# Two-stream cross-attention: the second-to-last batch's prompt values weighted on GpSimd and VectorE within the last batch, its projection placed earlier, and the last output stored in halves

## The chip, the cores and the metric

The kernel runs on one core of one Trainium2 chip. A core has TensorE (matrix products, results in the accumulation memory PSUM), VectorE, ScalarE and GpSimd (elementwise work in the on-chip memory SBUF; in this kernel VectorE and ScalarE read PSUM, GpSimd does not), and SyncE, which issues most transfers (DMA). Each engine works through its own queue in order, and waits on semaphores for the others. The metric is the time of one execution in device microseconds; the profile gives the time line of one profiled execution. In the profile's rows PE is TensorE, PEld its weight loads, DVE VectorE, ACT ScalarE, POOL GpSimd, SP SyncE; a q behind an engine's name is its sequencer, which issues and waits.

## The reference

There are 8 batches of 112 query rows with 320 channels (20 heads of 16), and for each batch 371 text tokens and 4 prompt tokens of 512 channels. For every head:

```
q = x @ W_q;  k, v = text @ W_k, text @ W_v;  k_ip, v_ip = prompts @ W_k_ip, prompts @ W_v_ip
probs_t  = softmax(q k^T / 4)                        # 112 x 371
text_out = probs_t @ v
qsem     = normalised(probs_t @ text)                # 512 channels
sem      = qsem @ normalised(prompts)^T              # 112 x 4
probs_ip = softmax(q k_ip^T / 4 + 0.5 * sem) * spatial_mask
out      = (text_out + probs_ip @ v_ip) @ W_out + b_out + x
```

All in float32. The norm of probs_t @ text is taken through the Gram matrix of the text tokens, so that the 512 channels are never formed for each query.

## The kernel before

**Tiling.** A batch's 20 heads are worked in five groups of four (`groups`, g = 0 to 4). For each group, `scores` makes the four score matrices, `probabilities` takes the maximum (VectorE, L678), the exponential (ScalarE, L682) and sends the probabilities through a DMA into the ring `xg` (L689); `transposed` turns them on VectorE (L701); `multiplied` takes the products with Gram matrix, prompt logits, a column of ones and values (`product`, L713) in 12 blocks; `reduced` (VectorE, L766) and `value_sums` (ScalarE, L740) take the results out of PSUM. In the last batch a part of the reductions goes through `shared`: copies on ScalarE (L750, L751), products on GpSimd (L755), sums on ScalarE (L759). `placed` (GpSimd, L632) puts a group's values beside the Gram matrix into the tile `u`; it must wait until TensorE is done with what stood there.

**Ends of batches.** What remains of a batch after its five groups is in `finish`, a generator that is advanced in pieces, each at a place written out by hand, between the products of the following batch. It divides the text part by the sums (`divided`, L812, GpSimd), makes the prompt weights w (L828 to L846), adds the weighted prompt values to the text part, turns the result (`ps_a`, copied to `aT`), projects it with W_out (`ps_o`, L896), adds input and bias (L902, VectorE) and stores it (L905).

For batches 0 to 5 the weighted prompt values are made on GpSimd: the batch's four prompt values are loaded to all 112 partitions (`prompt_values`, L591, 560 KB), multiplied by w (L874, 1280 elements a partition), and added up (L880 to L882). For batch 6 (`bd` given) it is done on TensorE: w is turned (L851), copied (L853), and multiplied with a table `bd` of 80 rows, one for each head and prompt, that holds the prompt's values in the head's own channels and zero elsewhere (L858, L865). `prompt_values_by_head` and `load_prompt_values_by_head` bring two such tables, for batches 6 and 7, through DRAM, and `own_channels` (L615, L618) clears what isn't a head's own.

**The last batch.** Batch 7 has no batch behind it, and its end is `ending`: the first 16 heads are divided and turned early; `bd` for batch 7 is turned (`ps_bT`, L963) and multiplied with W_out (`ps_bw`, L974), so that w, once turned (L1012), is multiplied with the projected table (L1015) into the same PSUM tile in which the text part's projection (L990) stands. One sum (L1019) and one store (L1020) follow.

**Order.** All five engines' queues are in the order of the program text. The order around the change is in `behind` (for batch 6's last group, where `finish(6)` is begun), in the loop over g of the last batch, and in the lines after it, which advance `ending(7)` (called `last`) and `finish(6)` (called `before`) in turns: of `finish(6)`, the turning of w comes after the first piece of `ending`, the two products into `ps_a` after the third, the projection L896 after the sixth, the sum L902 after the seventh, the store L905 after everything. GpSimd adds batch 7's input and bias (`with_bias`, L780) behind the cut of the tables in g = 1. PSUM tiles come from the pools mm, sc and qd; `bank(..., spare=True)` takes sc.

Of the kernel before, what the change touches and what calls it, by code (L numbers as in the profile page):

```python
# [20 lines left out]
def kernel(  # L21
# [209 lines left out]

    vipx = dram.tile([2, H, NIP, C], F32, tag="vipx", name="vipx", bufs=1)

# [362 lines left out]
    def prompt_values_by_head():  # L596

        nc.sync.dma_start(
            vipx,
            vipd[N - 2 * NIP :, :]  # L600
            .rearrange("(b n) c -> b n c", n=NIP)
            .unsqueeze(1)
            .to_broadcast([2, H, NIP, C]),
        )

    def load_prompt_values_by_head():
        t = io.tile([P, NT, E], F32, tag="ct", name="bd")
        st[B - 1]["xb"] = t[:S, 2, :C]
        bd = t[:HN, :2, :CP]
        nc.sync.dma_start(bd[:, :, :C], vipx.rearrange("b h n c -> (h n) b c"))  # L610
        return bd

    def own_channels(bd):

        nc.gpsimd.memset(bd[:, :, C:], 0.0)  # L615
        v = bd[:, :, :C].rearrange("p b (h d) -> p b h d", d=D)
        for sign, base in ((1, 0), (-1, NIP - 1)):
            nc.gpsimd.affine_select(  # L618
                out=v,
                in_=v,  # L620
                compare_op=ALU.is_ge,
                fill=0.0,
                base=base,
                pattern=[[0, 2], [-sign * NIP, H], [0, D]],
                channel_multiplier=sign,
            )
# [152 lines left out]
    def with_bias(b):  # L779
        nc.gpsimd.tensor_tensor(st[b]["xb"], x_sb[:, b, :], bias_sb, ALU.add)  # L780


    def finish(b, bd=None):

# [31 lines left out]
        if bd is not None:  # L816
            nc.vector.reciprocal(zr, z)
            divided()
        yield

        nc.scalar.activation(rn, rn, AF.Sqrt)
        nc.scalar.preload_act_table(AF.Exp)
        if bd is None:
            nc.vector.reciprocal(zr, z)
            divided()
        yield
# [21 lines left out]

        if bd is not None:
            ps = bank(f"ps_wT_{b}")  # L850
            nc.tensor.transpose(ps[:HN, :S], w.rearrange("s h n -> s (h n)"), ident[:S, :S])  # L851
            wT = work.tile([P, NE, TP], F32, tag="ctxT", name=f"wT_{b}")[:, 0, :S]
            nc.scalar.copy(wT[:HN], ps[:HN, :S])  # L853
            yield

            ps = bank(f"ps_a_{b}", spare=True)
            for i in range(NC):
                nc.tensor.matmul(  # L858
                    ps[:, i * S : (i + 1) * S],
                    attn[:, i * P : (i + 1) * P],  # L860
                    ident[:S, :S],
                    start=True,
                    stop=False,
                )
                nc.tensor.matmul(  # L865
                    ps[:, i * S : (i + 1) * S],
                    bd[:HN, i * P : (i + 1) * P],
                    wT[:HN],
                    start=False,
                    stop=True,  # L870
                )
        else:
            wv = work.tile([S, NIP, H, D], F32, tag="wv", name=f"wv_{b}", bufs=1)
            eng.tensor_tensor(  # L874
                wv,
                s["vip"],
                w.rearrange("p h n -> p n h").unsqueeze(3).to_broadcast([S, NIP, H, D]),
                ALU.mult,
            )
            eng.tensor_tensor(wv[:, :2], wv[:, :2], wv[:, 2:], ALU.add)  # L880
            eng.tensor_tensor(ah, ah, wv[:, 0], ALU.add)
            eng.tensor_tensor(ah, ah, wv[:, 1], ALU.add)  # L882
            yield

            ps = bank(f"ps_a_{b}", spare=True)
            for i in range(NC):
                nc.tensor.transpose(
                    ps[:, i * S : (i + 1) * S], attn[:, i * P : (i + 1) * P], ident[:S, :S]
                )
        aT = work.tile([P, NC, S], F32, tag="aT", name=f"aT_{b}")  # L890
        nc.scalar.copy(aT, ps[:, : NC * S].rearrange("p (i s) -> p i s", s=S))
        yield

        ps = bank(f"ps_o_{b}", spare=bd is not None)
        for i in range(NC):
# [13 lines left out]
    def ending(b, bd):  # L909
# [59 lines left out]

        ps_bw = bank("ps_bw")  # L970
        for i in range(NC):

            own = slice(i * RG, min((i + 1) * RG, HN))
            nc.tensor.matmul(  # L974
                ps_bw[own, :C], bT[:, i, own], wo_sb[:, i, :], start=True, stop=True
            )
        yield

        z2, rn = sm("z2"), sm("rn")
# [6 lines left out]

        turned_attention(range(FULL, NC))
        ps_o = bank(f"ps_o_{b}", spare=True)
        for i in range(NC):
            nc.tensor.matmul(  # L990
                ps_o[:S, :C], aT[:, i, :], wo_sb[:, i, :], start=(i == 0), stop=False
            )
        nc.vector.reciprocal(rn, rn)
# [20 lines left out]
        nc.scalar.copy(wT[:HN], ps[:HN, :S])  # L1014
        nc.tensor.matmul(ps_o[:S, :C], wT[:HN], bw, start=False, stop=True)  # L1015
        yield

        ob = work.tile([S, C], F32, tag="xb", name=f"ob_{b}", bufs=1)
        nc.vector.tensor_tensor(ob, ps_o[:S, :C], s["xb"], ALU.add)  # L1019
        nc.sync.dma_start(out[b], ob)  # L1020
        del st[b]
# [181 lines left out]
    def behind(n):  # L1203
# [73 lines left out]
        elif b % 2 == 0:  # L1277
# [6 lines left out]
            f(b - 1, 2)  # L1284
            run(("f", b), lambda: finish(b, bd=bd[:, 0]), 2)
        elif g == 1:
# [100 lines left out]
    drain(sums)  # L1387
    last = ending(b, bd[:, 1])
    next(last)
    run(before, None)  # L1390
    reduced(b, g, 0, 1)
    value_sums(b, g, 1)
    next(last)
    value_sums(b, g, 0, 1)
    reduced(b, g, 1)
    next(last)
    run(before, None)
    for _ in range(3):
        next(last)
    run(before, None)  # L1400
    next(last)
    run(before, None)
    drain(last)
# [44 lines left out]
```

## Time and profile before

| | |
|---|---|
| median of 3 runs | 428.86 us (424.92 to 431.55) |
| the profiled execution's own time | 426.6 us |
| its span, first to last instruction | 424.9 us |
| TensorE busy | 416.1 us, 98% |
| VectorE busy | 329.0 us, 77% |
| ScalarE busy | 185.9 us, 44% |
| GpSimd busy | 110.6 us, 26% |
| mean granted clock of TensorE | 0.997 |
| DMA | 64.27 MB, mean 151 GB/s |

All times in rows are from the span's start; the span leaves 1.7 us of the execution's own time outside. A row of the timeline reads: start, length, engine, line, operation, what it writes and reads, shape, count, and in brackets the idle time of the engine before it with what ended it. A row of the chain reads: start, length, what. A row of the stages reads: stretch, length, busy time of each engine with the count of instructions, granted clock, the DMA engines' share and rate.

### The profile page before, as it was taken

Reading aid. Unit: us, or ns where it says so; the run is one execution under the profiler, and the core shown is the slowest. Engines: PE = TensorE matmul, PEld = TensorE weight load, DVE = VectorE, ACT = ScalarE, POOL = GpSimd, SP = SyncE. Lnnn points to the kernel's source line nnn. Section 1 sums busy time; section 2 is a strip of 40 time slices with the busy share of each in tenths; the row PEclk is TensorE's granted clock in tenths of the full one; section 3 lists DMA queues with packets and bytes.
Section 4 is the critical chain, followed back from the end, with each engine's and each line's share of the span. In section 5 each row is a group of like instructions: output and inputs, shape, how many; then the busy total and the mean of one; then the engine's idle time right before and its main releaser. Section 6 shows DMA issues by size and latency. Waiting matters only on the chain.

```text
span 424.9 us, 14020 instructions
## 1 busy us (share of the span) xinstructions
PE 416.1 (98%) x5513; PEld 324.7 (76%) x5513; DVE 329.0 (77%) x681; ACT 185.9 (44%) x635; POOL 110.6 (26%) x271
## 2 busy tenths in 40 slices
PE   8999999999999999999999999999999999999995
PEld 8866586888677796879686887779776888777992
DVE  4055777877998887887889897797888897788963
ACT  3263243324633643424553454333633563356672
POOL 4303110031161342022061234003133226006440
PEclk9999999999999999999999999999999999999998
DMA  8677956778555656477645566586755435663400
GB/s 246 168 193 229 183 152 168 166 181 194 143 151 142 165 137 168 131 169 176 165 115 138 156 158 162 140 189 142 182 139 139 117 107 149 155 175 107 112 18 27
DMA packets 58254, 64.27 MB, mean 151 GB/s; under 512 B 19072, under 2 KB 52216, under 8 KB 58190
## 3 DMA queue, kind: packets, MB, share of 16 engines
q1 hardware_dynamic: 57498, 62.50, 58.8%
q8 instruction: 43, 0.70, 0.8%
q10 hardware_dynamic: 692, 0.89, 0.7%
q14 instruction: 21, 0.17, 0.1%
HBM read 18.67 MB, written 5.32 MB: 56 GB/s over the span
## 4 chain that ended last, share of the span: by engine, by line
PE 95%; DMA 1%; DVE 1%; ACT 1%; issue 0%; ACTq 0%; POOL 0%; SPq 0%; DVEq 0%; POOLq 0%
PE ps_qd L713 43%; PE ps_v L543 15%; PE ps_k L512 10%; PE ps_g L474 8%; PE ps_s L665 6%; PE ps_q L344 4%; PE ps_o L896 2%; PE ps_g L444 1%; DMA xg<-p 1%; PE ps_c L414 1%; PE ps_w L431 1%; PE ps_kv L280 1%; PE ps_k L526 1%; PE ps_k L503 1%; PE ps_x L336 0%
## 5 line engine op out<-in xcount | busy, mean ns | idle before, releaser
L713 PE MATMUL ps_qd<-u,xgT 32*112 32x232 f32 (+11 forms) x3840 | 218.1, 352 | 1.8 <-POOL u L632 1.3
L713 PEld LDWEIGHTS ps_qd<-u,xgT 32*112 32x112 f32 x3840 | 186.3, 172 | 33.1 <-issue 7.5
L701 DVE STREAM_TRANSPOSE xgT<-xg 128x768 f32<-128x768 f32 (+1 forms) x63 | 122.7, 1974 | 9.6 <-DMA xg<-p 9.1
L682 ACT ACTIVATE p<-ps_s,nmx 112x371 f32<-112x371 f32 x160 | 85.8, 585 | 50.1 <-DVE nmx L678 45.2
L766 DVE CUSTOM_DVE_ANT_0 junk<-ps_qd,p 112x371 f32<-112x371 f32 x150 | 81.2, 542 | 31.8 <-ACT pvs L740 10.9
L678 DVE TENSOR_REDUCE nmx<-ps_s 112x1 f32<-112x371 f32 x160 | 77.3, 536 | 22.3 <-PE ps_s L665 20.5
L632 POOL COPY u<-vr 128x64 f32<-128x64 f32 x120 | 26.9, 237 | 196.6 <-PE ps_qd L713 112.2
L543 PE MATMUL ps_v<-wv_sb,ctxT 128*128 128x384 f32 (+1 forms) x192 | 63.8, 479 | 0.3 <-ACT kT L519 0.3
L665 PE MATMUL ps_s<-kT,qm 32*112 32x375 f32 (+1 forms) x320 | 61.0, 486 | 0.0
L543 PEld LDWEIGHTS ps_v<-wv_sb,ctxT 128*128 128x128 f32 x192 | 35.3, 190 | 21.2 <-ACT kT L519 1.2
L740 ACT COPY pvs<-ps_qd 112x21 f32<-112x21 f32 x150 | 21.9, 199 | 62.1 <-DVE ss L766 60.9
L512 PE MATMUL ps_k<-ctxT,wk_sb 128*128 128x371 f32 x136 | 45.8, 481 | 0.0
L512 PEld LDWEIGHTS ps_k<-ctxT,wk_sb 128*128 128x128 f32 x136 | 24.6, 190 | 13.4 <-ACT ctxT L424 0.5
L474 PE MATMUL ps_g<-ctxT 128*32 128x119 f32 (+11 forms) x672 | 33.3, 344 | 0.0
L665 PEld LDWEIGHTS ps_s<-kT,qm 32*112 32x112 f32 x320 | 28.8, 171 | 4.0 <-issue 0.5
L474 PEld LDWEIGHTS ps_g<-ctxT 128*32 128x32 f32 x672 | 25.9, 109 | 7.4 <-issue 4.4
L550 ACT COPY vext<-ps_v 128x384 f32<-128x384 f32 (+1 forms) x24 | 11.2, 466 | 37.1 <-PE ps_v L543 37.0
L684 ACT COPY ipl<-ps_s 112x4 f32<-112x4 f32 x140 | 24.1, 172 | 0.0
L353 DVE TENSOR_SCALAR qm<-ps_q,emask 128x224 f32<-128x224 f32 (+1 forms) x25 | 8.9, 395 | 15.9 <-PE ps_q L344 15.9
L519 ACT COPY kT<-ps_k 128x371 f32<-128x371 f32 x17 | 8.0, 469 | 29.9 <-PE ps_k L512 29.9
L460 ACT ACTIVATE ug<-ps_g 128x375 f32<-128x375 f32 (+2 forms) x24 | 9.1, 378 | 27.4 <-PE ps_g L474 11.1
L402 DVE STREAM_TRANSPOSE ctxT<-ct 128x512 f32<-128x512 f32 x18 | 19.3, 1073 | 0.0
(159 smaller groups left out, 306.6 us busy)
## 6 DMA issues: line engine op xcount, KB each, us to landing
xg<-p SPq DMA_DIRECT2D x158, 162.3 KB
u<-ug SPq DMA_DIRECT2D x128, 99.0 KB
ct<-in_ctx_dram SPq DMA_DIRECT2D x24, 176.0 KB
vip<-vipd SPq DMA_DIRECT2D x6, 560.0 KB
vr<-vd SPq DMA_DIRECT2D x20, 120.0 KB
vd<-vext SPq DMA_DIRECT2D x14, 160.0 KB
vd<-vext SPq DMA_DIRECT2D x28, 40.0 KB
out_dram<-ob SPq DMA_DIRECT2D x8, 140.0 KB
```

Of the source, the lines that this page charges most:

```text
L474: nc.tensor.matmul(ps[p * RG : (p + 1) * RG, s0 : T - t0], ctxT[:, e, t0 + q * RG : t0 + (q + 1) * RG], ctxT[:, e, t0 + s0 : T], start=(e ...
L512: nc.tensor.matmul(ps[:, :TT], wk_sb[:, e, i * P : (i + 1) * P], s["ctxT"][:, e, :TT], start=(e == 0), stop=(e == NE - 1),)
L543: nc.tensor.matmul(ps[:, :w], ctxT[:, e, c * P : (c + 1) * P], wv_sb[:, e, :w], start=(e == 0), stop=(e == NE - 1),)
L632: nc.gpsimd.tensor_copy(region(b, c)[:, :, UV - c * P :], s["vr"][:, c * QN : (c + 1) * QN, g, :])
L665: nc.tensor.matmul(ps[:S, :w], qm[a * RG : (a + 1) * RG, i, r, j * S : (j + 1) * S], s["kT"][a * RG : (a + 1) * RG, i, :w], start=True, st ...
L678: nc.vector.tensor_reduce(nmx, ps[:S, :TT], AX.X, ALU.max, negate=True)
L682: nc.scalar.activation(p, ps[:S, :TT], AF.Exp, bias=nmx)
L684: nc.scalar.copy(s["ipl"][:, groups[g][a], :], ps[:S, TT:T])
L701: nc.vector.transpose(xT[:, j : j + n].rearrange("p j (k q) -> p q j k", q=QN), xg[:, :, j * RG : (j + n) * RG].rearrange("p q (j k) -> p ...
L713: nc.tensor.matmul(banks[a][:S, j * RG : UW], xT[a * RG : (a + 1) * RG, j, :S], region(b, c)[a * RG : (a + 1) * RG, p, q * RG :], start=(j ...
L740: nc.scalar.copy(s["pvs"][:, h, :], ps[:S, TT:UW])
L766: nc.vector.tensor_tensor_reduce(out=junk, in0=ps[:S, :TT], in1=s["p", g][:, a, :], scale=1.0, scalar=0.0, op0=ALU.mult, op1=ALU.add, accu ...
```

## The change

Batch 6's weighted prompt values are no longer made on TensorE with a table, but as in the batches before it, with two differences: the product with w is made in two halves of two prompts each (640 elements a partition, both on GpSimd, at two places of the last batch: behind the cut of the table in g = 1, and behind the first block of products in g = 3), and the three sums follow on VectorE, ahead of the transposition of the last group (g = 3, block 3). Its prompt values are loaded by `prompt_values(6)` when `finish(6)` is begun. Only batch 7's table remains: one table in DRAM, one load, one cut.

At the end, batch 6 needs only its three transpositions and the projection: the first are placed ahead of batch 7's first transpositions, the projection ahead of the fourth piece of `ending`; its sum follows batch 7's w on VectorE, and its store comes before batch 7's. In `ending`, `ps_bw` moves behind the turning of the last four heads, the last of the three products of the text part's projection moves behind the turning of w, and the last product, the sum and the store are made in two halves of 160 channels. Batch 7's input and bias are added on GpSimd after the fourth piece of `ending`. The division of batch 6 moves by one piece, behind the square root's issue.

```diff
-    vipx = dram.tile([2, H, NIP, C], F32, tag="vipx", name="vipx", bufs=1)
+    vipx = dram.tile([H, NIP, C], F32, tag="vipx", name="vipx", bufs=1)
...
-        bd = t[:HN, :2, :CP]
-        nc.sync.dma_start(bd[:, :, :C], vipx.rearrange("b h n c -> (h n) b c"))
+        bd = t[:HN, 0, :CP]
+        nc.sync.dma_start(bd[:, :C], vipx.rearrange("h n c -> (h n) c"))
...
-    def finish(b, bd=None):
+    def finish(b):
...
+        wv = work.tile([S, NIP, H, D], F32, tag="wv", name=f"wv_{b}", bufs=1)
+        by = w.rearrange("p h n -> p n h").unsqueeze(3).to_broadcast([S, NIP, H, D])
+        for some in (slice(0, 2), slice(2, 4)) if b == B - 2 else (slice(0, NIP),):
+            eng.tensor_tensor(wv[:, some], s["vip"][:, some], by[:, some], ALU.mult)
+            if b == B - 2:
+                eng = nc.vector if some.start else eng
+                yield
+        eng.tensor_tensor(wv[:, :2], wv[:, :2], wv[:, 2:], ALU.add)
+        eng.tensor_tensor(ah, ah, wv[:, 0], ALU.add)
+        eng.tensor_tensor(ah, ah, wv[:, 1], ALU.add)
+        yield
+
+        ps = bank(f"ps_a_{b}", spare=True)
+        for i in range(NC):
+            nc.tensor.transpose(
+                ps[:, i * S : (i + 1) * S], attn[:, i * P : (i + 1) * P], ident[:S, :S]
+            )
...
@@ ending
-        ps_bw = bank("ps_bw")
...
         turned_attention(range(FULL, NC))
+        ps_bw = bank("ps_bw")
...
+        projected(range(FULL))
...
         nc.scalar.copy(wT[:HN], ps[:HN, :S])
-        nc.tensor.matmul(ps_o[:S, :C], wT[:HN], bw, start=False, stop=True)
-        yield
-
+        projected(range(FULL, NC))
         ob = work.tile([S, C], F32, tag="xb", name=f"ob_{b}", bufs=1)
-        nc.vector.tensor_tensor(ob, ps_o[:S, :C], s["xb"], ALU.add)
-        nc.sync.dma_start(out[b], ob)
+        parts = [slice(i * C // 2, (i + 1) * C // 2) for i in range(2)]
+        for part in parts:
+            nc.tensor.matmul(
+                ps_o[:S, part], wT[:HN], bw[:, part], start=False, stop=part.stop == C
+            )
+        yield
+
+        for part in parts:
+            nc.vector.tensor_tensor(ob[:, part], ps_o[:S, part], s["xb"][:, part], ALU.add)
+            nc.sync.dma_start(out[b, :, part], ob[:, part])
...
@@ behind, batch 6
-            run(("f", b), lambda: finish(b, bd=bd[:, 0]), 2)
+            prompt_values(b)
+            f(b, 2)
...
@@ the last batch
             own_channels(bd)
-            with_bias(b)
+            run(before, None)
         for j, _ in enumerate(multiplied(b, g)):
             coming(g, places.get(g, {}).get(j, ()))
+            if g == 3 and j == 0:
+                run(before, None)
             if g == 3 and j == 3:
+                run(before, None)
                 placed(b, g + 1, (0,))
...
-    last = ending(b, bd[:, 1])
+    last = ending(b, bd)
     next(last)
-    run(before, None)
     reduced(b, g, 0, 1)
     value_sums(b, g, 1)
+    run(before, None)
     next(last)
     value_sums(b, g, 0, 1)
     reduced(b, g, 1)
     next(last)
     run(before, None)
-    for _ in range(3):
-        next(last)
-    run(before, None)
     next(last)
-    run(before, None)
+    with_bias(b)
+    next(last)
+    next(last)
+    run(before, None, 2)
     drain(last)
     drain(gens[before])
```

More of the change, by code (lines that the diff above doesn't have):

```diff
@@ L822, in finish @@
         nc.scalar.preload_act_table(AF.Exp)
-        if bd is None:
-            nc.vector.reciprocal(zr, z)
-            divided()
+        nc.vector.reciprocal(zr, z)
+        divided()
         yield
@@ L847, in finish @@
         yield
[L849 to L853, printed above, removed]
-            yield
[L856 to L878, printed above, removed]
-            )
[L880 to L889, printed above, removed]
@@ L892, in finish @@
         yield
-        ps = bank(f"ps_o_{b}", spare=bd is not None)
+        ps = bank(f"ps_o_{b}", spare=b == B - 2)
         for i in range(NC):
@@ L968, in ending @@
         yield
-        ps_bw = bank("ps_bw")
[L971 to L977, printed above, removed]
         z2, rn = sm("z2"), sm("rn")
@@ L987, in ending, with projected @@
         turned_attention(range(FULL, NC))
-        ps_o = bank(f"ps_o_{b}", spare=True)
[L989 to L992, printed above, removed]
+        ps_bw = bank("ps_bw")
+        for i in range(NC):
+            own = slice(i * RG, min((i + 1) * RG, HN))
+            nc.tensor.matmul(
+                ps_bw[own, :C], bT[:, i, own], wo_sb[:, i, :], start=True, stop=True
+            )
+        ps_o = bank(f"ps_o_{b}", spare=True)
+        def projected(chunks):
+            for i in chunks:
+                nc.tensor.matmul(
+                    ps_o[:S, :C], aT[:, i, :], wo_sb[:, i, :], start=(i == 0), stop=False
+                )
+        projected(range(FULL))
         nc.vector.reciprocal(rn, rn)
@@ L1014, in ending @@
         nc.scalar.copy(wT[:HN], ps[:HN, :S])
-        nc.tensor.matmul(ps_o[:S, :C], wT[:HN], bw, start=False, stop=True)
+        projected(range(FULL, NC))
+        ob = work.tile([S, C], F32, tag="xb", name=f"ob_{b}", bufs=1)
+        parts = [slice(i * C // 2, (i + 1) * C // 2) for i in range(2)]
+        for part in parts:
+            nc.tensor.matmul(
+                ps_o[:S, part], wT[:HN], bw[:, part], start=False, stop=part.stop == C
+            )
         yield
-        ob = work.tile([S, C], F32, tag="xb", name=f"ob_{b}", bufs=1)
-        nc.vector.tensor_tensor(ob, ps_o[:S, :C], s["xb"], ALU.add)
-        nc.sync.dma_start(out[b], ob)
+        for part in parts:
+            nc.vector.tensor_tensor(ob[:, part], ps_o[:S, part], s["xb"][:, part], ALU.add)
+            nc.sync.dma_start(out[b, :, part], ob[:, part])
         del st[b]
```

14 lines of the change are left out of this document (4 added, 10 removed).

## The prediction

> **What bounds the kernel now.** The page comes first: its span, then its chain of what ended last.
>
> ```profile
> span 424.9 us, 14020 instructions
> ...
> PE 95%; DMA 1%; DVE 1%; ACT 1%; issue 0%; ACTq 0%; POOL 0%; SPq 0%; DVEq 0%; POOLq 0%
> ```
>
> TensorE carries 95% of the chain, so over the whole kernel only work taken from TensorE, or a hole in its row, is worth anything. The diff touches the last batch, so next comes the chain in order of time, from 398 us on (start, length, what).
>
> ```profile
> 401.99 3.40 DMA xg<-p
> ...
> 405.52 1.61 DVE xgT L701
> ...
> 407.27 5.04 PE ps_qd L713 x87
> ...
> 414.38 0.54 DVE junk L766
> ...
> 416.00 1.08 PE ps_o L990 x4
> ...
> 417.87 1.62 PE ps_o L896 x6
> ...
> 419.98 0.81 PE ps_o L1015 x2
> ...
> 420.81 0.49 DVE ob L1019
> ```
>
> Here the picture differs from the average. The last group of heads waits for its probabilities (the DMA xg) and their transposition on VectorE (L701), then TensorE multiplies until 412.3, and from there to the end 12.6 us pass in a chain of small steps. One of them stands out: batch 6's output projection, L896, 1.62 us, lies between batch 7's projection and batch 7's last steps. The timeline shows whom it holds up.
>
> ```profile
> 417.89 0.30 DVE L1008 SCALAR_TENSOR_TENSOR w<-ex,sm_sb,rx 112x80 f32<-112x80 f32 x1
> 419.32 0.26 PE L1012 MATMUL ps_wT<-ident,w 112*80 112x112 f32 x1
> 419.68 0.25 ACT L1014 COPY wT<-ps_wT 80x112 f32<-80x112 f32 x1 [2.17 <-PE ps_wT L1012]
> ...
> 421.33 0.35 SPq L1020 DMA_DIRECT2D out_dram<-ob  x1
> 421.73 0.41 SPq L905 DMA_DIRECT2D out_dram<-ob  x1
> ```
>
> The prompt weights w are ready at 418.19, but TensorE turns them only at 419.32. And the last transfer that the kernel issues is batch 6's output (L905, 421.73), behind batch 7's. SyncE's own waits then give the landing:
>
> ```profile
> SPq L1443 <- DMA out_dram<-ob: 1.7, 2, 1.1
> ```
>
> Its last issue ends at 422.14; with 1.7 us of waiting the last store has landed at about 423.8, 2.1 us after its issue began. Some 1.1 us of closing follow to 424.9.
>
> **The change part by part: the end.** Up to w nothing on VectorE changes: its four reductions start with the end of the products and lead on to w.
>
> ```profile
> 412.19 0.55 DVE L766 CUSTOM_DVE_ANT_0 junk<-ps_qd,p 112x371 f32<-112x371 f32 x1 [1.21 <-PE ps_qd L713]
> ...
> 415.33 0.23 DVE L933 TENSOR_TENSOR attn<-pvs,zr 112x64 f32<-112x64 f32 x1
> ...
> 415.81 0.24 DVE L995 TENSOR_TENSOR fu<-pvs,rn 112x80 f32<-112x80 f32 x1
> ```
> ```profile
> 414.23 0.73 PE L974 MATMUL ps_bw<-wo_sb,bT 128*32 128x320 f32 x6
> 415.71 0.29 PE L948 MATMUL ps_a<-ident,attn 112*128 112x112 f32 x1 [0.75 <-DVE attn L933]
> ```
> ```profile
> 414.33 0.44 ACT L891 COPY aT<-ps_a 128x336 f32<-128x336 f32 x1 [0.72 <-PE ps_a L865]
> ```
>
> So w stays at 418.19, if TensorE has by then done what now precedes w. Batch 6's block there shrinks from one transposition and twelve products to three transpositions; with the two and three of batch 7 these take about 0.8 us (about 0.1 each), to 413.1. ScalarE's copy (0.44) ends by 413.3 to 413.6, and batch 6's projection, 1.62, by 414.9 to 415.2. The new wait is TensorE's for that copy; queued behind it is the transposition of the last four heads, which cannot start before VectorE's attn at 415.56 anyway: 0.4 us of cover. Behind that come the product ps_bw (0.73, moved from 414.23) and four entries of L990 (1.08): 416.0 + 0.73 + 1.08 = 417.8, 0.4 us before w. I cost both moves at nothing; past the cover, each 0.1 us would go straight to the end.
>
> TensorE follows VectorE by 0.15 us (attn 415.56, L948 415.71), so the turning of w moves from 419.32 to 418.34 and ScalarE's copy from 419.68 to 418.70, ending at 418.95. The last third of batch 7's projection, two entries of 0.27, now lies behind the turning of w, 418.46 to 419.0, beside that copy: free to within 0.1 us. The last product took 0.81 for two entries of 320 columns. In four entries of 160 I take 0.135 apiece: first half 419.0 + 0.81 - 0.27 = 419.54, second 419.81. For the sums: 320 columns take 0.49 (L1019), 80 take 0.24 (L995), a slope of 1.04 ns, so 160 take 0.32: 419.58 to 419.90 and 419.94 to 420.26. SyncE starts 0.03 behind the sum (L1019 ends at 421.30) and 0.4 behind its previous issue, so the last issue begins at 420.3. Batch 6's sum (0.49) follows w on VectorE, 418.2 to 418.7, where VectorE idles, and its store goes out at 418.75, early enough.
>
> The last store carries 70 KB in place of 140:
>
> ```profile
> 422.50:422.90 0.40, 0.00 (x0) 0.00 (x0) 0.00 (x0) 0.00 (x0) 0.00 (x0) 0.50 0.91 282
> ```
>
> At 282 GB/s, half the bytes save 0.25 us of the 2.1: landing at 420.3 + 1.85 = 422.15, against 423.8. **The end gains 1.6 us**, between 1.0 (both covers missed by 0.3) and 2.0.
>
> The Trainium skill's page "DMA: Bandwidth & Descriptors", § Anatomy of one DMA, puts nearly all of a transfer's time into a constant of about 2.0 us, with only the bytes over 436 GB/s on top (its fit is for transfers issued by GpSimd). By that an estimate for the half store is 2.2 us, the landing 422.5, and the end's gain 1.3. The trace's 2.1 us for 140 KB lies nearer to the constant than to the bytes.
>
> **The part within the batch.** Batch 6's weighting needs its prompt values, one more load of 560 KB in 0.5 us of SyncE's queue, behind four issues of xg.
>
> ```profile
> L689 SPq DMA_DIRECT2D xg<-p x4: 801/832/891, 378.8 to 381.7; - x4
> ```
> ```profile
> 383.80:386.30 2.50, 2.50 (x47) 2.39 (x43) 2.36 (x5) 1.86 (x8) 0.61 (x2) 1.00 0.05 15
> ```
>
> The fourth issue ends at 382.5, the next xg begins at 385.2, and in 383.8 to 386.3 the DMA engines are 5% busy: the load fits into the hole, and its reader comes at 393. Nothing; also for the smaller prompt table.
>
> GpSimd keeps one of batch 7's tables to cut out instead of two, and gets two half products of 640 elements; VectorE gets three sums (640, 320 and 320). The nearest rows:
>
> ```profile
> 352.06 2.47 POOL L874 TENSOR_TENSOR wv<-vip,w 112x1280 f32<-112x1280 f32 x1
> 354.61 1.55 POOL L880 TENSOR_TENSOR wv<-wv 112x640 f32<-112x640 f32 x1
> ```
> ```profile
> 391.34 2.08 POOL L618 TENSOR_SCALAR_AFFINE_SELECT bd<-bd 80x640 f32<-80x640 f32 x2
> 393.39 0.86 POOL L780 TENSOR_TENSOR bd<-x_sb,bias_sb 112x320 f32<-112x320 f32 x1
> ...
> 401.94 0.24 POOL L632 COPY u<-vr 128x64 f32<-128x64 f32 x1 [0.52 <-PE ps_qd L713]
> 404.77 0.24 POOL L632 COPY u<-vr 128x64 f32<-128x64 f32 x1 [2.59 <-PE ps_qd L713]
> 404.97 2.72 POOL L755 TENSOR_TENSOR shared<-shared,p 112x371 f32<-112x371 f32 x3
> ```
>
> A half product costs 1.24 (half of 2.47) to 1.55; I take 1.3, with the same operands. The first waits for batch 6's w, queued behind it the copies into u for group 2. It replaces about 1.0 of cutting out (half of 2.08) and 0.86 of bias, so GpSimd is free at about 394.8 against 394.25; the copies' reader starts at 396. The second falls into the hole of 2.59 before 404.77: 402.14 to 403.45. With the sums slope 1.04, 640 elements cost 0.82 and 320 cost 0.49 on VectorE: 403.5 to 405.4 with the gaps.
>
> ```profile
> 402.81 0.53 DVE L766 CUSTOM_DVE_ANT_0 junk<-ps_qd,p 112x371 f32<-112x371 f32 x1
> ...
> 405.52 3.02 DVE L701 STREAM_TRANSPOSE xgT<-xg 128x768 f32<-128x768 f32 x2 [2.16 <-DMA xg<-p]
> ```
>
> VectorE's own hole is 403.36 to 405.52, and the instruction queued behind the sums is L701 of the last group, on the chain above. The sums fit with 0.1 us to spare: zero if nothing disturbs them, and without cover each tenth is on the path. What can disturb them stands in these rows:
>
> ```profile
> 388.48 2.75 POOL L755 TENSOR_TENSOR shared<-shared,p 112x371 f32<-112x371 f32 x3 [0.22 <-ACT shared L751]
> ```
> ```profile
> 389.64 0.89 DVE L831 SCALAR_TENSOR_TENSOR fu<-fu,ipl 112x80 f32<-112x80 f32 x1
> ...
> 392.96 0.52 DVE L846 SCALAR_TENSOR_TENSOR w<-ex,sm_sb,rx 112x80 f32<-112x80 f32 x1
> ```
>
> Both have two inputs in SBUF. Alone such an operation takes 0.24 (L995) and 0.30 (L1008); beside GpSimd's products and cuts it took 0.89 and 0.52. L831 came through within the run of three GpSimd products, about where the second ends (0.92 apiece), not behind the third. I take from it that the two engines alternate: the third sum (from 404.87) meets the copy at 404.77 and perhaps one product. My value is +0.1; the ends are 0 and 2.7 (behind the whole run at 404.97).
>
> With less cutting out, L846 should be back at 0.30, 0.22 us sooner, and ScalarE waits for VectorE there (the maxima of the next scores). I credit 0.2, half of it lost to the missing cover at 405.4. **Within the batch: 0.0.**
>
> Sum: 1.6 us. The profiled execution took 426.6 us (span 424.9); it becomes 425.0 (423.3). The median of the runs, 428.86, lies 2.3 above that execution: 428.86 - 1.6 = **427.3 us**.
>
> **Rivals.** (1) *The port goes to GpSimd once.* The third sum waits for the copy and the first product, to 405.95, and ends at 406.3; L701 is 0.8 late, and TensorE after it: gain 0.8, 428.1. For it speaks L831's 0.89, against it that the sum asks before the product does. The Trainium skill's page "SBUF — State Buffer", § Who interferes with whom, says that a VectorE instruction with two SBUF inputs and a GpSimd instruction that reads SBUF exclude each other whole, the first to start winning. The trace agrees so far (0.89 against 0.24), and by that rule the order at 404.8 decides.
> (2) *Slower: GpSimd keeps the port through its queued run.* The third sum then waits for all three products, to 407.69, L701 starts at 408.1, 2.5 us late: 1.6 - 2.5 = 0.9 lost, 429.8. It decides once the sum is held past 407.1. Against it: L831 passed between two products.
> (3) *The end is shorter by less.* The half store lands no sooner than a whole one (2.1), and TensorE misses one cover by 0.3: gain 1.0, 427.9.
> (4) *Not first after all.* If ScalarE's copy of batch 6's attention comes behind its other copies and TensorE waits past 415.6, the projection stays in the path, and only the order of the stores is won: gain about 0.5, 428.4. The 0.4 us of cover speak against it.
>
> **How the numbers follow.** Forecast 0.60, rival (1) 0.17, (2) 0.07, (3) 0.11, (4) 0.05. All lie between 427 and 430 about the median. The runs of before reach from 424.92 to 431.55, so about 2% is what a measurement of this kernel can tell from no change. Range: from 427.3 - 3 to 429.8 + 1, 424.3 to 430.6; its width is mostly that spread. Within 2%: 0.91; faster 0.04 and slower 0.05, for mechanisms that no row shows.
>
> **What would show it.** Right: L1012 starts 0.15 behind w, SyncE's last issue is a half of batch 7, batch 6's store goes out right after w, the time from the last product (412.3) to the end is 1.6 us less; L846 at 0.30; three sums of 0.82, 0.49, 0.49 before L701, and L701 within 0.1 of its DMA. Wrong: a sum over 1 us, L701 waiting on VectorE, TensorE between 415.7 and 418.2 without a hole before the turning of w, or any shift ahead of 382 us.

## The result and the profile after

The changed kernel took 423.61 us in the median of 20 runs (421.6 to 427.64), the kernel before 426.39 in 20 runs beside it (423.46 to 431.55): a ratio of 0.9929, 95% interval 0.9909 to 0.9949. The forecast was 427.3 with a range from 424.3. The profiled execution went from 426.6 to 423.76 us, its span from 424.9 to 422.0. Two further comparisons gave 0.9953 (0.9924 to 0.9981) and 0.9924 (0.9895 to 0.9953). Weighted by their intervals the three make 0.9934 (0.9920 to 0.9948), so the change saves 2.2 to 3.4 us.

The page of the changed kernel, span and chain by engine:

```profile
span 422.0 us, 14010 instructions
...
PE 90%; DVE 4%; DMA 2%; SPq 1%; ACT 1%; POOL 1%; issue 1%; DVEq 0%; POOLq 0%
```

TensorE still carries the chain. The timeline of its end (start, length, engine, line, what, idle time before it):

```profile
416.76 0.30 DVE L979 SCALAR_TENSOR_TENSOR w<-ex,sm_sb,rx 112x80 f32<-112x80 f32 x1
416.98 0.48 DVE L871 TENSOR_TENSOR ob<-ps_o,xb 112x320 f32<-112x320 f32 x1
417.21 0.26 PE L983 MATMUL ps_wT<-ident,w 112*80 112x112 f32 x1 [0.41 <-DVE w L979]
417.49 0.34 SPq L874 DMA_DIRECT2D out_dram<-ob  x1
417.51 0.25 ACT L985 COPY wT<-ps_wT 80x112 f32<-80x112 f32 x1 [1.06 <-PE ps_wT L983]
417.85 0.76 PE L990 MATMUL ps_o<-bw,wT 80*112 80x160 f32 x4
418.70 0.56 DVE L996 TENSOR_TENSOR ob<-ps_o,bd 112x160 f32<-112x160 f32 x2 [1.24 <-PE ps_o L990]
419.06 0.79 SPq L997 DMA_DIRECT2D out_dram<-ob  x2
```

w ends at 417.06 (the row of L979) and TensorE turns it 0.15 us later; before, it did so 1.13 us later, behind batch 6's projection. Batch 6's store now goes out ahead of both of batch 7's. The halves did less than meant: both sums start only after both halves of the product, which end at 418.61.

The timeline within the last batch, where batch 6 is weighted:

```profile
390.67 0.98 DVE L675 TENSOR_REDUCE nmx<-ps_s 112x1 f32<-112x371 f32 x2
392.22 0.30 DVE L839 SCALAR_TENSOR_TENSOR w<-ex,sm_sb,rx 112x80 f32<-112x80 f32 x1
392.44 0.99 DVE L675 TENSOR_REDUCE nmx<-ps_s 112x1 f32<-112x371 f32 x2
392.61 1.33 POOL L845 TENSOR_TENSOR wv<-vip,w 112x640 f32<-112x640 f32 x1 [1.27 <-DVE w L839]
...
397.24 1.90 DVE L675 TENSOR_REDUCE nmx<-ps_s 112x1 f32<-112x371 f32 x4 [0.51 <-PE ps_s L662]
...
402.54 0.82 DVE L849 TENSOR_TENSOR wv<-wv 112x640 f32<-112x640 f32 x1
403.40 0.49 DVE L850 TENSOR_TENSOR attn<-attn,wv 112x320 f32<-112x320 f32 x1
403.82 0.24 POOL L629 COPY u<-vr 128x64 f32<-128x64 f32 x1 [1.31 <-PE ps_qd L710]
403.92 0.49 DVE L851 TENSOR_TENSOR attn<-attn,wv 112x320 f32<-112x320 f32 x1
404.01 2.98 POOL L752 TENSOR_TENSOR shared<-shared,p 112x371 f32<-112x371 f32 x3
404.57 1.59 DVE L698 STREAM_TRANSPOSE xgT<-xg 128x768 f32<-128x768 f32 x1 [0.16 <-DMA xg<-p]
```

The three sums take 0.82, 0.49 and 0.49 us and are over at 404.41; L698 starts at 404.57 and waits for its DMA, not for them. GpSimd's three products (L752) took 2.98 us where they took 2.72 before. And w of batch 6 (L839) takes 0.30, as forecast. The rows of before for the same place:

```profile
391.39 0.99 DVE L678 TENSOR_REDUCE nmx<-ps_s 112x1 f32<-112x371 f32 x2
393.40 0.98 DVE L678 TENSOR_REDUCE nmx<-ps_s 112x1 f32<-112x371 f32 x2
398.20 0.55 DVE L678 TENSOR_REDUCE nmx<-ps_s 112x1 f32<-112x371 f32 x1 [0.51 <-PE ps_s L665]
```

From the fourth group's first pair of maxima to its second pass 2.01 us before and 1.77 after; in all, from the fourth group's first maxima to the fifth's, 6.70 to 6.80 us in three traces of before and 6.56 to 6.59 in four of the changed kernel.

Laid side by side, the ends of all traces, in us. The first column runs from the start of the last group's maxima to the span's end. The others are pieces of it, one behind the other: from the start of the last group's products to the end of w, to the turning of w, to the end of the last sum, to the start of the last issue, to the span's end. In brackets stands how many products that nobody reads fill the hole (below).

| kernel | whole end | products to w | w to its turning | turning to last sum | sum to last issue | issue to span's end |
|---|---|---|---|---|---|---|
| before, 3 traces | 26.64 to 26.68 | 10.93 | 1.13 | 1.98 | 0.43 | 3.15 |
| changed, 4 traces | 24.78 to 24.91 | 10.75 (once 10.89) | 0.15 | 2.05 | 0.21 | 2.57 |
| end alone | 25.26 | 11.06 | 0.31 | 1.99 | 0.21 | 2.62 |
| weighting alone | 28.03 | 10.75 | 2.64 | 2.03 | 0.43 | 3.08 |
| last product whole | 24.98 | 10.90 | 0.15 | 1.98 | 0.03 | 2.88 |
| larger table back | 24.91 | 10.76 | 0.15 | 2.05 | 0.21 | 2.67 |
| stores in the old order | 25.77 | 10.75 | 0.15 | 2.05 | 0.82 | 2.95 |
| projection late | 28.82 | 10.89 | 4.03 | 2.04 | 0.21 | 2.57 |
| two tiles, two queues | 24.39 | 10.75 | 0.15 | 1.78 | 0.03 | 2.59 |
| weighting, hole filled (5) | 27.15 | 10.91 | 1.66 | 2.03 | 0.43 | 3.07 |
| weighting, hole filled (3) | 26.54 | 10.75 | 1.21 | 2.03 | 0.43 | 3.06 |
| projection late, hole filled (8) | 27.67 | 11.79 | 2.00 | 2.05 | 0.21 | 2.57 |
| projection late, hole filled (4) | 25.91 | 10.75 | 1.31 | 2.05 | 0.21 | 2.56 |

The end gives about 1.86 us (26.66 to 24.80) and the fourth group 0.2: 2.06 us. Over all pairs of traces the two are 1.73 to 1.90 and 0.11 to 0.24.

### The profile page after: what moved, and what is told of

Read it like the earlier page. It is cut to its first block, busy times and chain, and to the rows that moved or that the text cites. A ratio compares the mean times of both kernels' runs of the same rounds, so it can differ in the third digit from the quotient of the medians.

```text
span 422.0 us, 14010 instructions
## 1 busy us (share of the span) xinstructions
PE 413.7 (98%) x5505; PEld 323.6 (77%) x5505; DVE 330.9 (78%) x685; ACT 185.4 (44%) x634; POOL 112.1 (27%) x273
## 4 chain that ended last, share of the span: by engine, by line
PE 90%; DVE 4%; DMA 2%; SPq 1%; ACT 1%; POOL 1%; issue 1%; DVEq 0%; POOLq 0%
PE ps_qd L710 42%; PE ps_v L543 15%; PE ps_k L512 10%; PE ps_g L474 8%; PE ps_s L662 6%; PE ps_q L344 3%; PE ps_o L865 2%; PE ps_g L444 1%; DVE xgT L698 1%; DMA vr<-vd 1%; DVE nmx L675 1%; PE ps_c L414 1%; DVE junk L763 1%; DMA ct<-in_ctx_dram 1%; PE ps_k L503 1%
## 5 line engine op out<-in xcount | busy, mean ns | idle before, releaser
L698 DVE STREAM_TRANSPOSE xgT<-xg 128x768 f32<-128x768 f32 (+1 forms) x63 | 122.6, 1970 | 6.7 <-DMA xg<-p 5.9
```

What stands on the lines that cost most here:

```text
L698: nc.vector.transpose(xT[:, j : j + n].rearrange("p j (k q) -> p q j k", q=QN), xg[:, :, j * RG : (j + n) * RG].rearrange("p q (j k) -> p ...
```

## The experiments

**The two kernels once more.**

> The changed kernel once more, unaltered. Theory 1 (the gain is the end's, and the 1.35 us that the changed kernel's profile is ahead by 95 us are chance in how the first loads land): ratio 0.994 to 0.996, and the maxima of batch 1, group 2 start anywhere between 92.5 and 94.5 us. Theory 2 (the 1.35 us belong to the change, through the smaller table or other addresses in DRAM): ratio 0.991 to 0.994, and that start again at 92.9, 1.3 below the kernel before.

> The kernel before once more, unaltered: it measures what chance does. Ratio 1.000 within 0.002. Theory 1: the maxima of batch 1, group 2 start up to 1.3 us away from the 94.17 of the first profile. Theory 2: they start at 94.2 within 0.2.

> The changed kernel with the table of both prompts still in DRAM and loaded (200 KB each way in place of 100), one of them never used and never cut out. Theory 1 (the gain lies in the end and chance in the loads): ratio as the changed kernel's, 0.994 to 0.996, the end's stretch unchanged within 0.05. Theory 2 (the smaller table gives about 1 us somewhere ahead of the last batch): 0.9965 to 0.998.

```diff
-    vipx = dram.tile([H, NIP, C], F32, tag="vipx", name="vipx", bufs=1)
+    vipx = dram.tile([2, H, NIP, C], F32, tag="vipx", name="vipx", bufs=1)
...
-        bd = t[:HN, 0, :CP]
+        bd = t[:HN, :2, :CP]
```

Measured: the changed kernel 425.12 us against 427.12 (0.9953, 0.9924 to 0.9981), the kernel before 426.19 (0.9991, 0.9958 to 1.0024); with the larger table back 422.86 against 426.25 (0.9938, 0.9903 to 0.9974). In the first two traces the changed kernel led by 1.3 us from 95 us on, long before the last batch, where only the smaller table could have made a difference. That lead is chance: the variants of the changed kernel issue the same work up to there, and yet the third group's maxima of batch 1 start anywhere from 92.23 to 96.35 (VectorE's timeline of the projection late with eight products and of the stores in the old order):

```profile
92.23 1.43 DVE L675 TENSOR_REDUCE nmx<-ps_s 112x1 f32<-112x371 f32 x3
```
```profile
96.35 0.99 DVE L675 TENSOR_REDUCE nmx<-ps_s 112x1 f32<-112x371 f32 x2
```

The repeat of before stood at 92.81, that of the changed kernel at 95.55. The theory that the smaller table moves something early falls: the kernel with the larger table is no slower.

**The end without the weighting, and the weighting without the end.**

> Batch 6 is weighted on TensorE with its table as before; only the end is the changed one (projection first, store order, halves, place of ps_bw). Theory 1: TensorE's block at the end is 1.2 us longer than in the changed kernel and the projection of batch 6 ends at about 416.5 in place of 415, so about 0.3 to 0.9 of the end's 1.9 us is lost again: ratio 0.9965 to 0.9975. Theory 2: the table is as large as before, so the early 1.3 us are missing, ratio as in theory 1 and the early start at 94.2.

> Batch 6 is weighted on GpSimd and VectorE as in the changed kernel, one table, but the end is the old one: projection behind batch 7's, whole product, batch 6's store last. Theory 1: only the reductions' spacing (0.2 us) is gained, and up to 0.4 lost within the batch: ratio 0.999 to 1.001. Theory 2: the early 1.3 us come with the smaller table: ratio 0.996 to 0.998, early start at 92.9.

```diff
-        nc.tensor.matmul(ps_o[:S, :C], wT[:HN], bw, start=False, stop=True)
...
+        projected(range(FULL, NC))
...
+        for part in parts:
...
-    for _ in range(3):
-        next(last)
-    run(before, None)
+    run(before, None, 2)
```

(The diff is that of the end alone, against the kernel before; the weighting alone has the other half.) Measured: the end alone 424.71 us against 427.12 (0.9958, 0.9927 to 0.9989), the weighting alone 426.92 (0.9991, 0.9958 to 1.0024). So most of the gain is in the end. In the traces the end alone has 1.40 us of the 1.86: its w comes 0.13 later than in the kernel before (0.31 later than in the changed one) and is turned after 0.31, since batch 6's twelve small products still stand on TensorE ahead of it. The weighting alone showed something that neither theory had. Here are its timeline on TensorE, and two stretches of it (length, busy time of PE, PEld, DVE, ACT, POOL with counts, granted clock, DMA share, GB/s):

```profile
415.16 0.29 PE L917 MATMUL ps_a<-ident,attn 112*128 112x112 f32 x1 [1.45 <-DVE attn L902]
415.29 2.70 PE L959 MATMUL ps_o<-wo_sb,aT 128*112 128x320 f32 x6
417.78 2.60 PE L865 MATMUL ps_o<-wo_sb,aT 128*112 128x320 f32 x6
420.21 0.26 PE L981 MATMUL ps_wT<-ident,w 112*80 112x112 f32 x1
```
```profile
414.80:418.20 3.40, 3.04 (x8) 1.79 (x9) 2.21 (x9) 2.13 (x5) 0.00 (x0) 0.68 0.00 0
418.20:421.60 3.40, 3.01 (x9) 1.39 (x7) 0.49 (x1) 0.25 (x1) 0.00 (x0) 0.82 0.00 0
```

Behind TensorE's idle 1.45 us the granted clock falls, and six entries (MATMUL instructions of the trace) of 320 columns take 2.60 us where they take 1.78 at full clock. So w waits 2.64 us here; at full clock the same order makes it wait 1.21 us (below).

**The halves, the order of the stores, the place of the projection.**

> The changed kernel with the last product, sum and store whole again (one product of 320 columns, one sum, one store of 140 KB). By the prediction's step the half store lands 0.25 us sooner for its bytes and is issued 0.2 sooner: the stretch from the turning of the last w to the end, 4.83 us in the changed kernel, becomes 5.1 to 5.3. By the changed kernel's trace, where the first sum waits for both halves, the halves win nothing at the sum: 4.85 to 4.95, all of it from the landing. Ratio 0.995 to 0.997 in both.

```diff
-        parts = [slice(i * C // 2, (i + 1) * C // 2) for i in range(2)]
+        parts = [slice(0, C)]
```

> The changed kernel with batch 6's store issued last again, behind batch 7's two halves. If the order of the stores is a term of its own, SyncE's last issue begins 0.4 us later and lands in 2.1 in place of 1.7: the stretch from the last sum to the end, 2.78 in the changed kernel, grows by 0.6 to 0.9. If landings overlap so far that the order is free: below 0.2.

```diff
     next(last)
-    run(before, None, 2)
+    run(before, None)
     drain(last)
```

> The changed kernel with batch 6's projection back behind batch 7's and ahead of the turning of w. If the place of the projection is the main term, the turning of w starts 1.1 to 1.3 us behind w in place of 0.15, and the stretch from w to the end grows by 1.0 to 1.2 us; ratio 0.997 to 0.999. The rival (the earlier stores alone make the gain): at most 0.3 longer.

```diff
     next(last)
-    run(before, None)
     next(last)
...
-    run(before, None, 2)
+    run(before, None, 3)
```

Measured against 426.25: the last product, sum and store whole 424.52 (0.9957, 0.9931 to 0.9984), stores in the old order 424.71 (0.996, 0.9929 to 0.9992), projection late 425.89 (0.9974, 0.9942 to 1.0006). By time none is told from the changed kernel; the traces price them, with one trace each. The timeline of the kernel with the product whole:

```profile
417.69 0.27 PE L983 MATMUL ps_wT<-ident,w 112*80 112x112 f32 x1 [0.41 <-DVE w L979]
...
419.18 0.49 DVE L996 TENSOR_TENSOR ob<-ps_o,bd 112x320 f32<-112x320 f32 x1 [1.24 <-PE ps_o L990]
419.70 0.32 SPq L997 DMA_DIRECT2D out_dram<-ob  x1
```

From the turning of w to the span's end it takes 4.89 us, with halves 4.83: the halves are worth 0.06. That is less than two traces of the same end differ: the kernel with the larger table has the same halves and takes 4.93, with 2.67 from the last issue to the end in place of 2.57. The halves' sums end 0.07 later and the second issue waits 0.18 longer for the first; only the time behind the last issue is shorter, by 0.31 (2.57 against 2.88). With batch 6's store issued last, the timeline ends so:

```profile
422.42 0.56 DVE L996 TENSOR_TENSOR ob<-ps_o,bd 112x160 f32<-112x160 f32 x2 [1.24 <-PE ps_o L990]
422.77 0.97 SPq L997 DMA_DIRECT2D out_dram<-ob  x2
423.79 0.42 SPq L874 DMA_DIRECT2D out_dram<-ob  x1
```

The time from the last sum to the span's end is 3.77 against 2.78: the order of the stores is worth 1.0 us. And with the projection late, the clock fell again (row of the stages, then TensorE's timeline):

```profile
414.80:418.20 3.40, 3.40 (x7) 1.99 (x7) 0.55 (x2) 0.23 (x1) 0.00 (x0) 0.50 0.00 0
```
```profile
412.88 0.45 PE L917 MATMUL ps_a<-ident,attn 112*128 112x112 f32 x1 [2.37 <-DVE attn L902]
...
416.74 2.84 PE L865 MATMUL ps_o<-wo_sb,aT 128*112 128x320 f32 x6
```

**Halves that do not wait for each other.**

> The changed kernel with the very last product's halves in two PSUM tiles (each half's sums over the chunks, too: twice as many entries of 160 columns), and the first half's store issued by ScalarE's queue, the second's by SP's. In the changed kernel the first half's sum starts only after both halves of the product (418.70, both ended by 418.61). If that wait is one for the tile that both halves share, the first sum here starts beside the second half's product, 0.2 us or more before that product's end, the second sum ends 0.1 to 0.3 us earlier behind w's turning than in the changed kernel (2.05 us from the turning's start to the last sum's end there, 1.75 to 1.95 here), and the last issue comes 0.03 us behind the last sum and not 0.21: 4.83 us from the turning's start to the span's end become 4.3 to 4.6. Rival: the sums wait for the later half here too, since the halves end within 0.15 us of each other, and the doubled entries cost as much: 4.8 us again. The time is the changed kernel's or up to 0.5 us less (ratio to before 0.9945 to 0.9957).

```diff
-        ps_o = bank(f"ps_o_{b}", spare=True)
...
+        ps_o = [bank(f"ps_o_{b}_{i}", spare=i == 0) for i in range(2)]
...
-            nc.sync.dma_start(out[b, :, part], ob[:, part])
...
+            eng.dma_start(out[b, :, part], ob[:, part])
```

Measured 423.8 us against 426.21 (0.9948, 0.9921 to 0.9974). Its timeline:

```profile
418.53 0.75 PE L995 MATMUL ps_o<-bw,wT 80*112 80x160 f32 x4
419.11 0.56 DVE L999 TENSOR_TENSOR ob<-ps_o,bd 112x160 f32<-112x160 f32 x2 [0.97 <-PE ps_o L995]
419.46 0.37 ACTq L1000 DMA_DIRECT2D out_dram<-ob  x1
419.69 0.32 SPq L1000 DMA_DIRECT2D out_dram<-ob  x1
```

The first sum starts at 419.11, before the product's second half has ended (419.28), the last issue comes 0.03 behind the last sum, and from the turning to the span's end pass 4.40 us instead of 4.83. So the first sum's wait was one for the tile that both halves shared. In time, 0.4 us cannot be told apart; that this kernel beats the changed one is not shown.

**A filled hole.** In TensorE's idle stretch ahead of batch 7's last turning stand products with the identity that nobody reads.

> The weighting without the new end, as before, and in TensorE's idle 1.45 us ahead of batch 7's last turning five products of 256 columns with the identity, which nobody reads (about 1.1 us of work). Without them the granted clock was 0.68 in 414.80 to 418.20, the six entries of 320 columns of batch 6's projection took 2.60 us (1.78 in the changed kernel), and w's turning waited 2.64 us behind w. Theory clock: the idle stretch brings the half clock; here the granted clock stays 1.00 through the end, the entries take 1.8 us, the wait behind w falls to 1.0 to 1.4 us, and the time to a ratio of 0.995 to 0.997 (0.9991 without). Theory chance: the low clock falls where it likes; the granted clock drops below 0.9 somewhere between 410 and the last product again, the wait stays over 2 us and the ratio near 0.999.

> The changed kernel with batch 6's projection behind batch 7's instead of in TensorE's hole, and in that hole, of 2.37 us, eight products of 256 columns with the identity that nobody reads (about 1.7 us of work). Without them the granted clock was 0.59 in 411.40 to 414.80 and 0.50 in 414.80 to 418.20, and w's turning waited 4.03 us behind w. Theory clock: a filled hole keeps the clock; granted 1.00 up to the last product, w's turning 1.0 to 2.4 us behind w (the projection's 1.78 us stand ahead of it), the time 0.5 to 1.5 us under the one without the products (ratio 0.9974 there, 0.994 to 0.996 here). Theory chance: a clock below 0.9 between 410 and 418 again, a wait over 3 us, and a ratio near 0.9974.

> The same as the weighting with filled hole, but three products that nobody reads and not five. Five held the granted clock at 1.00, but each took two entries of 0.22 us, 2.43 us in all and not the 1.1 us planned, so that batch 7's last turning came 0.9 us late, which ate what the clock gave. Three take 1.33 us, within the idle 1.45 us. Theory clock: granted clock 1.00 up to the last product, runs whose record of the clock is 0.996 or lower 0 to 3 of 12 (7 of 12 without the products, 2 with five), w's turning 0.9 to 1.7 us behind w, and a ratio of 0.994 to 0.997 (0.9991 without, 1.0015 with five). Theory chance: low records in half of the runs again, and a ratio of 0.998 to 1.000. Third: entries that nobody reads cost time wherever they stand (clock full and yet a ratio over 0.999).

> The same as the late projection with filled hole, but four products that nobody reads and not eight, which took 3.72 us and held up batch 7's last turning by 1.1 us or more. Four take 1.8 us behind the copy of bT, within the hole of 2.37 us but for 0.2 us. Theory clock: granted clock 1.00 up to the last product, low records (0.996 or lower) in 0 to 4 of 12 runs (10 of 12 without the products, 3 with eight), w's turning 1.2 to 2.2 us behind w, 26.0 us from the start of the last maxima to the end (28.8 without, 27.7 with eight, 24.9 in the changed kernel), and a ratio of 0.995 to 0.998. Theory chance: low records in most runs again, ratio 0.9974 or more. Third: the products cost time wherever they stand: ratio 1.000 or more at full clock.

```diff
+        for i in range(3):
+            nc.tensor.matmul(
+                ps[:P, 2 * P : 4 * P], ident, wk_sb[:, 0, : 2 * P], start=True, stop=True
+            )
```

(Weighting alone, three products; the others have five, and in the projection late eight or four behind the copy of bT.) With five and eight the ratios were 1.0015 (0.9987 to 1.0043) and 1.0028 (1.0003 to 1.0053): the products took two entries each, twice what I had planned (2.43 us for the five), and held up the turning of batch 7's last heads. With three and four they were 0.9993 (0.9954 to 1.0032) and 0.9986 (0.9951 to 1.0022). The weighting with three, TensorE's timeline and the stage:

```profile
413.81 1.56 PE L947 MATMUL ps_bT<-wk_sb,ident 128*128 128x256 f32 x6
415.34 0.29 PE L917 MATMUL ps_a<-ident,attn 112*128 112x112 f32 x1
415.47 2.04 PE L963 MATMUL ps_o<-wo_sb,aT 128*112 128x320 f32 x6
417.34 1.78 PE L865 MATMUL ps_o<-wo_sb,aT 128*112 128x320 f32 x6
```
```profile
414.80:418.20 3.40, 3.39 (x14) 1.89 (x13) 2.35 (x11) 2.23 (x5) 0.00 (x0) 1.00 0.00 0
```

The granted clock stays at 1.00 and the six entries of L865 take 1.78 us; all four kernels with a filled hole have it so. One stretch of 3.41 us at half clock takes 0.004 from the mean of a run of 425 us. A mean granted clock of 0.996 or less was recorded in:

| kernel | hole open | hole filled, too long | hole filled, fitting |
|---|---|---|---|
| weighting alone | 7 of 12 | 2 of 12 | 3 of 12 |
| projection late | 10 of 12 | 3 of 12 | 2 of 12 |

In the kernel before it was 22 of 132 runs, in the changed kernel 5 of 38. So the hole brings the low clock, and what fills it keeps the clock up. Both expected ratios were nevertheless missed (0.9993 for 0.994 to 0.997, 0.9986 for 0.995 to 0.998): what the full clock saves in the traces is not found again in the medians. By the traces there was little to find in the first, whose end at full clock (26.54) is only 0.1 us shorter than before's; in the second the interval holds the expected ratios. What the low clock costs in time stays open: runs with a low record were longer (427.55 us in the mean of 7 against 425.08 of 5 in the weighting alone, 426.19 of 10 against 425.67 of 2 in the projection late), but a hole that brings it also costs time by itself. What the two traces do give is the price of the projection's place at full clock: 25.91 against 24.80, 1.1 us.

**One more pair of the kernels.**

> The changed kernel once more, beside the kernel before. Two accounts of its gain stand. The end alone: from the start of the maxima of batch 7's fifth group to the span's end both traces of before take 26.7 us and both of the changed kernel 24.8 to 24.9, and nothing else differs for good, so 1.8 us, a ratio of 0.9957, as in the two calls so far (0.9953 and, with the product whole, 0.9957). A second gain outside of the end, of about 1 us, that the runs so far missed: a ratio of 0.993 as in the first comparison (0.9929). In the trace the stretch from those maxima to the end is 24.8 to 24.9 us by both.

> The kernel before, for one more trace. Its median lies 2.4 to 2.8 us over the changed kernel's (ratios 0.9929, 0.9953, 0.9924), of which the two kernels' ends give 1.8 in the traces so far (26.7 against 24.8 to 24.9 us from the start of the last maxima to the span's end). Theory end alone: this trace has 26.7 us there and its other stretches within the spread of the others (174.7 to 175.4 from batch 1's third group to batch 5, 97.2 to 97.4 up to batch 7, 16.8 to 18.0 for its first two groups, 13.9 to 14.4 for the next two). Theory of a second place: one of these stretches is 0.5 us or more over the changed kernel's in this trace.

> The changed kernel, for one more trace, as a pair to the kernel before. Theory end alone: 24.8 to 24.9 us from the start of the last maxima to the span's end, and the stretches ahead within the same spread as the kernel before's. Theory of a second place: one of the stretches ahead is 0.5 us or more under the kernel before's.

The repeat gave 423.58 us against 426.21 (0.9924, 0.9895 to 0.9953), on the side of a second gain; its trace and the last pair have the same ends as the others. The last pair, one execution each of 425.85 (before) and 424.95 us, has one stretch 0.8 us apart: from the third group's maxima in batch 7 to the fifth's, 14.85 before and 14.04 after. But 0.7 of that lies in the first half, where the other traces of both kernels scatter from 7.45 to 7.86; the fourth group's 0.1 to 0.2 is what every pair has.

## Why the prediction was wrong in size and right in mechanism

- **The median.** The forecast was counted from 428.86, three runs' median; twenty runs have 426.39. The prediction saw that the profiled execution (426.6) lay 2.3 us lower and counted from the median all the same. From 426.39 its own sum gives 424.8, inside its range. This step failed, and it is the larger part of the miss (2.5 of 3.7 us). The range's low end, "427.3 - 3", hung on the same centre, so the measured 423.61 lies below it. (The range's high end is added wrongly: 429.8 + 1 is 430.8, not 430.6; nothing rests on it.)
- **The end gains 1.6.** From w's end to the span's end the time fell from 6.68 to 4.98 us, by 1.7. The turning of w came at 0.15 behind w (0.98 gained, as forecast), with the projection in the hole and the copy at 411.82, whose end did not hold the last turning up. The rest had two errors that nearly cancelled, so that the 1.6 came out so near is partly luck. The last issue was forecast 2.11 us behind w and came at 2.41: the first sum did not start with the first half, since both halves share a tile, and SyncE's second issue follows its first by 0.4. Against that, the time from the last issue to the end fell by 0.58 and not 0.25; 0.27 of it comes with a whole store too (3.15 to 2.88), so that part is not in the bytes.
- **Up to w nothing on VectorE changes.** This step failed too: VectorE's last four reductions start 0.70 us apart instead of 0.73, and w ends 5.71 us behind the products instead of 5.89, in all four traces (in one the products themselves ran 0.14 longer). The spacing goes with the weighting: the end alone, which keeps batch 6's twelve small products on TensorE, has 0.73 and the weighting alone 0.70. By what way these products reach VectorE was not tried.
- **Within the batch: 0.0.** This step failed. The 0.22 us of batch 6's w were won as forecast, but nothing of it was lost: the last sum ended 0.10 to 0.16 us ahead of L698's start in all four traces, and the fourth group is 0.2 shorter. With the reductions this makes 1.7 + 0.18 + 0.2, about 2.1 us instead of 1.6.
- **Rivals.** (1) and (2) did not happen: the third sum began at 403.92 and kept its 0.49 us, and GpSimd's run of three products, begun at 404.01, took 0.26 us longer (its first product 1.24 us instead of 0.98). This agrees with the Trainium skill's page "SBUF — State Buffer", § Who interferes with whom, by which the first to start wins. (For (1), the prediction's own figures end the sum at 406.4, 405.95 + 0.49, and not at 406.3.) (3) did not happen: behind the last issue the half store took 2.57 us and the whole one 2.88, and TensorE missed no cover. What it doubted came in another way: the sums and issues of the halves lost most of that again. (4) did not happen; its price, 1.1 us, was right by the traces at full clock (25.91 against 24.80).
- **What stays open.** The three comparisons together say 2.2 to 3.4 us, the traces 2.1; their centre, 2.8, leaves 0.7 us without a place. Single runs of the same work lie up to 4 us apart by batch 1's third group, so the difference may be chance; that is not shown.

## What to carry to other kernels

Count a forecast from many runs of the kernel before, or from the profiled execution, and let the range hold the centre's own uncertainty. A short hole on TensorE is a place for work that waits anyway, and filling it also kept the granted clock up, though products that nobody reads won no time by it. Cutting the last product, sum and store in halves won nothing that could be told here, while both halves lay in one PSUM tile; which store is issued last was worth 1.0 us.

## What the runs showed of the hardware

The granted clock went to half for one or two stretches of about 3.4 us, and idle times of TensorE far shorter than that stood beside the fall: 1.45 us ahead of it (weighting alone) and 2.37 us around it (projection late). The kernel with the end alone had it within the batch, behind a stretch in which TensorE was busy for 1.67 of 3.50 us:

```profile
394.80:398.30 3.50, 1.67 (x45) 1.59 (x41) 3.50 (x5) 2.87 (x14) 0.48 (x2) 1.00 0.49 137
398.30:401.70 3.40, 3.40 (x31) 3.39 (x27) 1.86 (x5) 1.67 (x7) 2.71 (x3) 0.52 0.19 55
```

The length of an idle time is not what decides: 1.65 us (weighting with three products, at 44.31) and 1.66 us (projection late with eight, at 184.09) left the clock at 1.00. What comes nearer is how long TensorE was busy in the 3.41 us just ahead of the fall: 1.58 us (end alone, from 395.05), 1.68 (weighting alone, from 412.59) and 1.89 (projection late, from 408.62). In the stretches of that grid with the two idle times that changed nothing it was busy for 1.81 and 1.75 us. So in these traces the border lies near half of a stretch, and it is not sharp.

The Trainium skill's page "TensorE: Matmul & The Clock Gate", § Part 1: The HAM clock gate, describes a free-running window of 3413 ns and a half clock after an idle window. The length agrees (0.50 in 398.46 to 401.88 with the end alone, 1.00 on both sides), the condition does not: in none of these windows was TensorE idle throughout, so here partly idle windows already sufficed.
